# First attention of a two-layer gated cross block: roots taken by logarithm and exponential, bias rows spread by TensorE, and the opening's keys dealt out anew between VectorE and GpSimd

## The chip, the cores and the metric

The kernel runs on one core of one Trainium2 chip. The metric is the device time of one execution in microseconds (us); the time before is the median of three runs. Engines are named as the profile names them: PE (TensorE, with PEld its weight loads), DVE (VectorE), ACT (ScalarE), POOL (GpSimd) and SP (SyncE). ACTq and SPq are the instructions by which ACT and SP start transfers (DMAs).

## The reference, cut to what matters

Four sequences of 256 tokens with 256 features go through two layers. Each layer has a cross attention to a context of 1601 tokens, then a feed-forward part, each behind a gate. The change touches the first attention alone:

```python
def _ln(t, w, b):                       # over the 16 features of a head
    m = jnp.mean(t, axis=-1, keepdims=True)
    v = jnp.var(t, axis=-1, keepdims=True)
    return (t - m) * jax.lax.rsqrt(v + EPS) * w + b        # EPS = 1e-6
...
q = _ln((x @ Wq + bq).reshape(b, s1, H, HD), qn_w, qn_b)   # H = 16 heads, HD = 16
kv = jnp.concatenate([y_main @ Wk + bk, y_main @ Wv + bv], axis=-1).reshape(b, s2, H, 2 * HD)
k = _ln(kv[..., :HD], kn_w, kn_b)
v = kv[..., HD:]
ctx = _attn(qT, k.transpose(0, 2, 1, 3), v.transpose(0, 2, 1, 3))
# and a second attention to the last 16 context tokens (k_dca, v_dca), added to ctx
return ctx @ Wo + bo
```

So every key and every query of every head needs one reciprocal root of a variance. `y_main` has 1585 tokens.

## The kernel before, in words

**Stages.** By the profile's time axis: an opening that prepares the first sequence (0 to about 86 us), the first attention (to about 600 us), then the first feed-forward part, the second attention and the second feed-forward part. Each stage's instructions are issued in the order in which the program text makes them: `keep_order` ties every instruction of an engine to the one before it, on PE, ACT, DVE, POOL and SP. Nothing is rearranged later, so an instruction that waits holds up all that stands behind it on its engine. The pools' buffers add waits of their own: `ps_s` has three buffers of PSUM, `ps_m` and `ps_o` one each, the raw keys `kn` two, the split keys `kp` two.

**DMA lanes.** The transfers share eight completion counters, dealt out in turn. The ninth transfer waits, on the engine that issues it, until the first has landed, and so on.

**Keys.** The 13 tiles of 128 context tokens form the groups [0,1,2], [3,4,5], [6,7,8], [9,10,11], [12]. For a group the kernel multiplies the context by `wkv` (keys and values side by side), adds the key bias, squares (ACT), sums per head and scales to a variance (DVE), takes the root, scales the keys (POOL), and splits them into three bf16 parts by two rounds of "ACT rounds, POOL subtracts" (`split`, L341 to L352). `key_turn` (L516) then transposes the three parts into `kTs` by one DMA per tile, started by SP. Key weights, query weights and biases have their mean over a head removed first (`center`, L326), so that the products come out with zero mean.

**Roots.** In the opening `deviations` (L827) scales the variance and calls `newton_rsqrt` (L354): two integer instructions for a first guess and three rounds of three instructions, all on DVE. In the steady part `scale_heads` (L374) calls `pool_rsqrt` (L363): the two integer instructions on DVE, then three rounds of four on POOL, in the space of the squares `sq`; the scaling of the keys (L388) is POOL's too.

**The opening** (L817 to L949) makes all keys of sequence 0 at once. `first_pair` (L482) projects two tiles into one `ps_s` buffer. Groups 0 and 1 are scaled and split by POOL, group 2 is scaled by POOL and split by DVE, groups 3 and 4 by POOL. Biases and the short weight rows arrive as DMAs that write one row to all 128 partitions (`partition_broadcast`). Queries of sequence 0 are projected, scaled, staged as 64-row bf16 blocks (`stage_queries`, POOL) and transposed by a DMA (`turn_queries`). Then 16 `greatest_tile` calls find the greatest score of each query for the first slab (a sequence and four heads); `CHUNKS` cuts the keys by groups 0, 1, 2 and 3 with 4. `shift` works it into the queries, which are turned once more for the attention itself.

**The steady part** (L950 to L1024) walks 16 slabs of 14 slots. A slot runs one or two `greatest_tile` calls for the next slab (PE L647, DVE L654), one `attend_tile` (PE L686, then the exponential on ACT, L694), every second time a `weigh` (PE L708), and then whatever `plan` holds for the slot: key projections of the next sequence (PE L475, DVE L477, ACT L478), the steps of `scale_heads` and `split`, query steps, output projections. A key group that begins in slot s squares in s, sums and takes the root in s+1, scales in s+3, splits in s+4 and s+6 and is turned in s+7:

```python
for o, step in zip((1, 3, 4, 6), steps[1:]):
    place(plan, slot + o, [step])
place(plan, slot + 7, [lambda: key_turn(b, gi)])
```

Sequence 1 is prepared during the slabs of sequence 0, and so on; sequence 3 needs no successor.

Of the kernel before, what the change touches and what calls it, by code (L numbers as in the profile page):

```python
# [9 lines left out]
F32 = mybir.dt.float32  # L10
# [49 lines left out]
def tile_gated_cross_blocks(ctx: ExitStack, tc: tile.TileContext, a: dict, out: bass.AP):  # L60
# [11 lines left out]
    def load_x(t, queue=nc.sync):  # L72
        queue.dma_start(out=xs[t], in_=a["x"][t * P : (t + 1) * P, :])
# [189 lines left out]
    with ExitStack() as ph:  # L263
# [12 lines left out]
        def load_group(b, gi):  # L276
# [6 lines left out]

        wkv = wp.tile([P, 2 * D], F32, name="wkv")
        bkv = wp.tile([P, 2 * D], F32, name="bkv")
        nc.sync.dma_start(out=wkv[:, :D], in_=a["L0_xattn_Wk"])
        nc.scalar.dma_start(out=wkv[:, D:], in_=a["L0_xattn_Wv"])
        fetched = {(0, 0): load_group(0, 0)}
        nc.scalar.dma_start(out=bkv[:, :D], in_=a["L0_xattn_bk"].partition_broadcast(P))
        load_x(0)  # L290
        nc.scalar.dma_start(out=bkv[:, D:], in_=a["L0_xattn_bv"].partition_broadcast(P))
        load_x(1)
        fetched[0, 1] = load_group(0, 1)
        wq = load(wp, "wq0", [P, DC, D], a["L0_xattn_Wq"].rearrange("(c p) n -> p c n", p=P), nc.scalar)
        bq = bcast_row(wp, "L0_xattn_bq", D, nc.scalar)
        fetched.update({(0, gi): load_group(0, gi) for gi in range(2, 4)})
        hn = {
            n: bcast_row(wp, f"L0_xattn_{n}", HD0, nc.sync if "dca" in n else nc.scalar)
            for n in ("qn_w", "qn_b", "kn_w", "kn_b", "kn_dca_w", "kn_dca_b")
        }  # L300
        early = ph.enter_context(ExitStack())
        lp = early.enter_context(tc.tile_pool(name="l0last", bufs=1))
# [23 lines left out]
        def center(t3):  # L326

            g = t3.shape[1]
            sm = small.tile([P, 2 * H], F32, name="cen", bufs=2)
            nc.vector.reduce_sum(sm[:, :g], t3, axis=AX.X)  # L330
            nc.vector.tensor_scalar_mul(sm[:, :g], sm[:, :g], 1.0 / HD0)
            nc.vector.tensor_tensor(t3, t3, bc_last(sm[:, :g], HD0), ALU.subtract)
# [21 lines left out]
        def newton_rsqrt(v, y, t):  # L354

            nc.vector.tensor_scalar(y.bitcast(I32), v.bitcast(I32), 1, None, ALU.arith_shift_right)
            nc.vector.tensor_scalar(y.bitcast(I32), y.bitcast(I32), -1.0, 1597463007.0, ALU.mult, ALU.add)
            for k in range(3):
                nc.vector.tensor_tensor(t, y, y, ALU.mult)
                nc.vector.scalar_tensor_tensor(t, t, -0.5, v, ALU.mult, ALU.mult)  # L360
                nc.vector.scalar_tensor_tensor(v if k == 2 else y, t, 1.5, y, ALU.add, ALU.mult)

        def pool_rsqrt(v, y, t):  # L363

            nc.vector.tensor_scalar(y.bitcast(I32), v.bitcast(I32), 1, None, ALU.arith_shift_right)
            nc.vector.tensor_scalar(y.bitcast(I32), y.bitcast(I32), -1.0, 1597463007.0, ALU.mult, ALU.add)
            for k in range(3):
                nc.gpsimd.tensor_tensor(t, y, y, ALU.mult)
                nc.gpsimd.tensor_tensor(t, t, v, ALU.mult)
                nc.gpsimd.tensor_scalar(t, t, -0.5, 1.5, ALU.mult, ALU.add)  # L370
                nc.gpsimd.tensor_tensor(v if k == 2 else y, t, y, ALU.mult)

        def scale_heads(src, n, g):

            sq = hp.tile([P, GN * H, HD0], F32, name="sq", bufs=1)
            v = small.tile([P, GN * H], F32, name="hn_var", bufs=2)[:n, :g]

            def square():
                nc.scalar.activation(sq[:n, :g], src, AF.Square)

            def rsqrt():
                nc.vector.reduce_sum(v, sq[:n, :g], axis=AX.X)
                nc.vector.tensor_scalar(v, v, 1.0 / HD0, 1e-6, ALU.mult, ALU.add)
                space = sq.rearrange("p g e -> p (g e)")[:n]
                pool_rsqrt(v, space[:, :g], space[:, g : 2 * g])

            def scale():
                nc.gpsimd.tensor_tensor(src, src, bc_last(v, HD0), ALU.mult)  # L388

            return [square, rsqrt, scale]  # L390
# [379 lines left out]
        def plan_keys(plan, b, base, at, l):  # L770

            ctxg, kns = {}, {}
            for gi, g in enumerate(groups):

                def fetch(gi=gi):
                    ctxg[gi] = fetched.pop((b, gi), None) or load_group(b, gi)

                place(plan, base + max(at[0][0], at[gi][0] - 8), [fetch])
                for i, slot in enumerate(at[gi]):
                    place(plan, base + slot, [lambda gi=gi, i=i: key_project(b, gi, ctxg[gi], kns, i)])  # L780

                def begin(gi=gi, slot=base + l[gi]):
                    steps = key_parts(gi, kns)
                    steps[0]()
                    for o, step in zip((1, 3, 4, 6), steps[1:]):
                        place(plan, slot + o, [step])
                    place(plan, slot + 7, [lambda: key_turn(b, gi)])

                place(plan, base + l[gi], [begin])
# [25 lines left out]


        FIRST = 2 * GN  # L817
        nk0, ns0 = NKT * H * HD0, (NKT - FIRST) * H * HD0
        kn0 = kTs_f[1][:, :nk0].rearrange("p (g e) -> p g e", e=HD0)
        sq0 = kTs_f[1][:, nk0 : nk0 + ns0].rearrange("p (g e) -> p g e", e=HD0)  # L820
        v0 = lp.tile([P, (NKT + QT + 1) * H], F32, name="v0")
        qcol, dcol = FIRST * H, (NKT + QT) * H

        def kcol(t):
            return (t if t < FIRST else t + QT) * H

        def deviations(c0, c1):  # L827
            v = v0[:, c0:c1]
            nc.vector.tensor_scalar(v, v, 1.0 / HD0, 1e-6, ALU.mult, ALU.add)
            y, t = (lp.tile([P, NKT * H], F32, name=f"nr_{k}")[:, : c1 - c0] for k in "yt")  # L830
            newton_rsqrt(v, y, t)

        def square(t0, t1, base):

            for n, lo, hi in ((P, t0, min(t1, NKT - 1)), (TMAIN, NKT - 1, t1)):
                if lo < hi:
                    nc.scalar.activation(sq0[:n, (lo - base) * H : (hi - base) * H], kn0[:n, lo * H : hi * H], AF.Square)

        def sum_squares(t0, t1):
            for n, lo, hi in ((P, t0, min(t1, NKT - 1)), (TMAIN, NKT - 1, t1)):  # L840
                if lo < hi:
                    nc.vector.reduce_sum(
                        v0[:n, kcol(lo) : kcol(hi - 1) + H], sq0[:n, (lo - t0) * H : (hi - t0) * H], axis=AX.X
                    )

        def parts(gi, eng):
# [4 lines left out]
            v = v0[:n, kcol(g[0]) : kcol(g[-1]) + H]  # L851
# [3 lines left out]
                [lambda: nc.gpsimd.tensor_tensor(src, src, bc_last(v, HD0), ALU.mult)] + steps + [lambda: key_turn(0, gi)]  # L855
# [9 lines left out]
        group = [parts(gi, nc.vector if gi == 2 else nc.gpsimd) for gi in range(len(groups))]  # L865
        zero_padding(vps[0])
        center(kv3[0])
        next(ln0)
        center(kv3[1])
# [11 lines left out]
        square(0, 4, 0)  # L881
        center(wq.rearrange("p c (h e) -> p (c h) e", e=HD0))
        center(bq.rearrange("p (h e) -> p h e", e=HD0))
        first_pair(4, kn0)
        square(4, FIRST, 0)
        for i in range(QT):
            query_project(0, i)
        sqq = hp.tile([P, GN * H, HD0], F32, name="sq", bufs=1)[:, : QT * H]
        nc.scalar.activation(sqq, q3, AF.Square)
        sum_squares(0, FIRST)  # L890
        nc.vector.reduce_sum(v0[:, qcol : qcol + QT * H], sqq, axis=AX.X)
        deviations(0, qcol + QT * H)
        step(group[0])
        step(group[1])
        fetched[0, 4] = load_group(0, 4)
        first_pair(6, kn0)
        step(group[0])
        nc.vector.tensor_tensor(q3, q3, bc_last(v0[:, qcol : qcol + QT * H], HD0), ALU.mult)
        affine, fold, first_split, second_split = query_parts(0)[3:]
        affine()  # L900
        first_pair(8, kn0)
        step(group[0])
        step(group[0])
        fold()
        first_split()
        first_pair(10, kn0)
        step(group[1])
        second_split()
        stage_queries(0, 0)
        turn_queries((0, 0), 0)  # L910
        first_pair(12, kn0)
        square(FIRST, NKT, FIRST)
        step(group[1])
        step(group[1])
        sum_squares(FIRST, NKT)
        deviations(qcol + QT * H, dcol)
# [15 lines left out]
        deviations(dcol, dcol + H)  # L932
        for g in GREATEST[8:12]:
            greatest_tile(0, *g)
        next(last)
# [12 lines left out]
        nc.scalar.activation(gate, gate, AF.Tanh)  # L948
        early.close()  # L949
# [19 lines left out]
        for u, (b, s) in enumerate(slabs):  # L969
# [3 lines left out]
            if s == 0 and b + 1 < B:  # L973
                plan_keys(plan, b + 1, base_slot, KEYS[b > 0], PARTS_AT[b > 0])
                iterate(plan, base_slot + 32, last_tokens(b + 1), 12)
                if b == 0:
                    plan_queries(plan, 1, base_slot, [0, 3, 9, 10], [13, 14], [15, 16, 18, 19, 20, 21, 23])
                if b + 2 < B:
                    plan_queries(
                        plan, b + 2, base_slot + NS * SLOTS, [-8, -6, -4, -3], [-2, -1], [0, 1, 3, 4, 6, 8, 10]  # L980
                    )
# [667 lines left out]
```

## Time and profile before

| what | us |
|---|---|
| median of three runs (lowest, highest) | 1640.45 (1640.38, 1642.27) |
| profiled execution, own time | 1644.6 |
| its span, first to last instruction | 1642.8 |
| PE busy in the span | 1542.2 (94%) |
| DVE, ACT, POOL busy | 1170.4, 788.0, 658.1 |
| stretch 0 to 86 us (opening), first score product of the opening | 47.44 |
| stretch 86 to 330 us: PE busy | 221.7 of 244 |
| stretch 330 to 570 us: PE busy | 227.1 of 240 |
| stretch 560 to 1643 us: PE busy | 1061.5 of 1083 |

A row of the timeline gives the start in us, the duration in us, engine, line, operation, what it writes and reads with shapes, how many instructions were merged, and in brackets the idle time before it with what ended it. "PEclk" is the granted TensorE clock, 1.00 being full. Waits are rows of "engine, what waited, <-, what it waited for: total us, times, longest".

### The profile page before, as it was taken

The page shows a single profiled execution, that of the slowest core. Times are in us where ns is not written, and L with a number is a line of the kernel's source. Part 1 is how long each engine was busy: PE and PEld are TensorE (multiplying, and loading weights), DVE is VectorE, ACT ScalarE, POOL GpSimd, SP SyncE. Part 2 cuts the span into 40 slices and gives each one's busy share as a digit, 9 for nine tenths or more (in the row PEclk, how much of TensorE's full clock was granted, in tenths as well). Part 3 has the DMA queues.
Part 4 walks back from the last instruction along what each step waited for, and adds up shares of the span by engine and source line. Part 5 has one row for each costly group of instructions (what it writes and reads, how often), then busy time and mean ns, then how long its engine had stood idle before and what let it go on. Part 6 is the DMA issues. An engine that isn't in the chain of part 4 may idle for free.

```text
span 1642.8 us, 34188 instructions
## 1 busy us (share of the span) xinstructions
PE 1542.2 (94%) x13274; PEld 924.6 (56%) x13282; DVE 1170.4 (71%) x2621; ACT 788.0 (48%) x1808; POOL 658.1 (40%) x754
## 2 busy tenths in 40 slices
PE   4598899899999999998999999999999999999998
PEld 1254454454455554445666666666666666666665
DVE  6876668767767736677777777777877777877655
ACT  2144545554555553453555444544455444454443
POOL 4534414513621215534445444444445444444410
PEclk8699899999999999999999999999999999999999
DMA  3512612430424132000000000010000000000000
GB/s 102 100 35 45 94 32 45 78 57 16 87 44 95 37 90 110 1 2 2 15 9 21 9 15 15 8 21 3 15 9 15 15 15 15 9 2 2 2 0 27
DMA packets 148466, 54.06 MB, mean 33 GB/s; under 512 B 133200, under 2 KB 143952, under 8 KB 148176
## 3 DMA queue, kind: packets, MB, share of 16 engines
q1 hardware_dynamic: 134592, 50.65, 14.6%
q10 hardware_dynamic: 13712, 1.23, 0.6%
q8 instruction: 104, 1.70, 0.4%
q14 instruction: 58, 0.48, 0.1%
HBM read 24.30 MB, written 1.05 MB: 15 GB/s over the span
## 4 chain that ended last, share of the span: by engine, by line
PE 77%; DVE 13%; ACT 3%; issue 2%; POOL 2%; DMA 1%; ACTq 0%; SPq 0%; DVEq 0%; POOLq 0%
PE ps_o L1426 21%; PE ps_sc L1363 20%; PE ps_s L686 6%; PE ps_s L647 6%; PE ps_o L708 5%; DVE mxs L654 4%; PE ps_y L1444 4%; PE ps_m L1352 3%; PE ps_m L475 2%; PE ps_v L1186 2%; ACT pr L1378 1%; PE ps_a L1200 1%; PE ps_g L1557 1%; PE ps_x L1131 1%; PE ps_y L1582 1%
## 5 line engine op out<-in xcount | busy, mean ns | idle before, releaser
L1413 POOL TENSOR_TENSOR pr<-pr,rs 128x1604 f32<-128x1604 f32 x128 | 364.2, 2867 | 434.9 <-DMA rs<-ws 393.2
L1426 PE MATMUL ps_o<-pT,cx 128*128 128x256 f32 x1664 | 372.2, 381 | 7.8 <-DVE pT L1419 7.8
L1370 DVE CUSTOM_DVE_ANT_0 pr<-ps_sc,mk 128x401 f32<-128x401 f32 x512 | 294.6, 576 | 95.0 <-PE ps_sc L1363 56.2
L1363 PE MATMUL ps_sc<-ctxT,qT 128*32 128x401 f32 x4096 | 359.5, 502 | 0.4 <-DVE nm L1370 0.4
L1378 ACT ACTIVATE pr<-pr,nm 128x401 f32<-128x401 f32 x512 | 321.3, 629 | 71.0 <-DVE nm L1370 70.3
L1426 PEld LDWEIGHTS ps_o<-pT,cx 128*128 128x128 f32 x1664 | 318.0, 191 | 52.2 <-DVE pT L1419 8.5
L654 DVE TENSOR_REDUCE mxs<-ps_s 128x2 f32<-128x768 f32 (+1 forms) x256 | 245.9, 979 | 78.5 <-PE ps_s L647 77.9
L694 ACT ACTIVATE e<-ps_s 128x1024 f32<-128x1024 f32 (+1 forms) x224 | 214.7, 963 | 176.0 <-PE ps_s L686 161.5
L1419 DVE STREAM_TRANSPOSE pT<-pr 128x1664 f32<-128x1664 f32 x128 | 242.9, 1899 | 4.9 <-POOL pr L1413 4.7
L1363 PEld LDWEIGHTS ps_sc<-ctxT,qT 128*32 128x32 f32 x4096 | 126.2, 110 | 204.4 <-issue 119.5
L647 PE MATMUL ps_s<-kT,qTs 64*128 64x384 bf16 (+1 forms) x1536 | 177.6, 346 | 40.4 <-DMA qTs<-qp 18.1
L686 PE MATMUL ps_s<-qTs,kT 64*128 64x256 bf16 x2496 | 176.1, 272 | 11.0 <-DVE mxs L654 11.0
L686 PEld LDWEIGHTS <-kT 64*128 64x128 bf16 x2496 | 125.8, 95 | 57.5 <-issue 23.6
L647 PEld LDWEIGHTS <-qTs 64*128 64x128 bf16 x1536 | 67.0, 97 | 138.4 <-issue 91.4
L708 PE MATMUL ps_o<-e,vp 128*32 128x256 f32 x1664 | 112.8, 390 | 0.0
L1395 ACT ACTIVATE ws<-ws 32x32 f32<-32x32 f32 x64 | 14.6, 228 | 194.3 <-DVE ws L1394 194.3
L1436 ACT COPY ao<-ps_o 128x256 f32<-128x256 f32 x64 | 23.9, 373 | 152.5 <-PE ps_o L1426 141.3
L1378 ACT ACTIVATION_READ_ACCUMULATOR pr<-pr,nm 128x1 f32 x512 | 95.4, 186 | 0.0
L1444 PE MATMUL ps_y<-vo,ao 128*128 128x256 f32 x256 | 73.3, 409 | 2.1 <-ACT ao L1436 2.1
L1444 PEld LDWEIGHTS ps_y<-vo,ao 128*128 128x128 f32 x256 | 43.9, 191 | 46.5 <-ACT pr L1378 39.9
L708 PEld LDWEIGHTS ps_o<-e,vp 128*32 128x32 f32 x1664 | 44.6, 110 | 43.0 <-issue 25.6
L1352 PE MATMUL ps_m<-xnT,aq 128*128 128x256 f32 x256 | 65.8, 380 | 0.0
(288 smaller groups left out, 1553.9 us busy)
## 6 DMA issues: line engine op xcount, KB each, us to landing
ctxT<-in_ctxT_dram SPq DMA_DIRECT2D x4, 800.5 KB, 8.0
ctxg<-in_ctxT_dram SPq DMA_DIRECT2D x16, 192.0 KB, 3.2
kT<-in_L_xattn_Wq_dram SPq DMA_DIRECT2D x4, 512.0 KB, 3.5
wo<-in_L_xattn_Wo_dram SPq DMA_DIRECT2D x4, 512.0 KB, 4.5
bq<-nm SPq DMA_DIRECT2D x128, 2.0 KB, 1.7
bq<-nm ACTq DMA_DIRECT2D x128, 2.0 KB, 2.0
rs<-ws SPq DMA_DIRECT2D x128, 1.0 KB, 1.9
rs<-ws ACTq DMA_DIRECT2D x128, 1.0 KB, 1.8
```

Source lines behind the costliest of these rows:

```text
L647: nc.tensor.matmul(ps[:, k, :w], lhsT=qT[rows, j, i, r, :], rhs=kT[rows, 2 * s + r, c0 : c0 + w], start=j == 0, stop=j == NP - 1,)
L654: nc.vector.tensor_reduce(greatest_of[u][:, i, 2 * r : 2 * r + 2, n], ps[:, :, :w], AX.X, ALU.max)
L686: nc.tensor.matmul(ps[:, k, jj * S : (jj + 1) * S].rearrange("p (i q) -> p i q", i=QT), lhsT=kT[rows, 2 * s + r // 2, (j + jj) * P : (j + ...
L694: nc.scalar.activation(e[:, :, : nj * S], ps[:, :, : nj * S], AF.Exp)
L708: nc.tensor.matmul(summed[u][(r + k) * W : (r + k + 1) * W, :S], lhsT=vps[b % 2][:, j + jj, h * VW : h * VW + W], rhs=made[u, j, r][:, k, ...
L1363: nc.tensor.matmul(ps[i * TQ : (i + 1) * TQ, :KS], lhsT=queries[u][:, t * TQ : (t + 1) * TQ], rhs=ctxT[b][:, i * KS : (i + 1) * KS], start ...
L1370: nc.vector.tensor_tensor_reduce(out=prs[u % 3][:, t, :KS], in0=ps[:, :KS], in1=masks[b], scale=-1.0, scalar=3.0e38, op0=ALU.add, op1=ALU. ...
L1378: nc.scalar.activation(p, p, AF.Exp, bias=found[u][:, 0, t : t + 1], scale=-1.0, accum_out=found[u][:, 1, t : t + 1])
L1413: nc.gpsimd.tensor_tensor(p, p, bc_last(factors[:, ts], KS), ALU.mult)
L1419: nc.vector.transpose(pTs[u % 2][:, ts].rearrange("p t k -> p (t k)"), prs[u % 3][:, ts].rearrange("p t k -> p (t k)"))
L1426: nc.tensor.matmul(po[:, u % 2], lhsT=contexts[b][:, k, :], rhs=pTs[u % 2].rearrange("p t (k q) -> p t k q", q=TQ)[:, :, k, :], start=k == ...
L1444: nc.tensor.matmul(ys[b][:, i], lhsT=outs[u][:, i * P : (i + 1) * P], rhs=vo[:, h, :], start=(h, i) == (0, 0), stop=(h, i) == (H - 1, QT - 1),
```

## The change

All of it lies in the first attention.

- The activation table set that holds logarithm and exponential together is loaded as ACT's first instruction, and once more after the `Tanh` of the gates.
- `newton_rsqrt` and `pool_rsqrt` are gone. `log_root` takes Ln and then Exp with scale -0.5 on ACT; `newton` does one round of three instructions on DVE.
- A group's steps in the steady part become square (s), variance (s+1, DVE), root (s+2, ACT), one Newton round on DVE with the scaling on POOL (s+3), and the rest as before. The root's scratch is no longer the squares' space. For queries, a step is put in the same way.
- The biases of key, value and query and four short rows are loaded into one row on one partition (seven DMAs of ACT's queue), and spread to all partitions by two matmuls with a row of ones (512 and 320 columns); DVE centres the key bias from PSUM, ACT copies the rest out. Query weights and query bias lie in one tile and are centred together.
- The second x tile moves from SP's queue to ACT's; the order of the opening's loads changes.
- In the opening, groups 0 and 1 are scaled and split by DVE alone, groups 2, 3 and 4 by POOL alone; squares, sums and roots of groups 0, of the queries, of group 1 and of the rest are taken in four portions (before: groups 0 and 1 with the queries, then the rest); the last 24.5 KB of keys are fetched after the first queries are turned.

```diff
+        nc.scalar.preload_act_table_set("natural_log_exp_and_others")
...
+        def load_row(at, name):
+            n = a[name].shape[0]
+            nc.scalar.dma_start(out=row[:, at : at + n], in_=a[name].unsqueeze(0))
...
-        nc.scalar.dma_start(out=bkv[:, :D], in_=a["L0_xattn_bk"].partition_broadcast(P))
+        load_row(0, "L0_xattn_bk")
+        load_row(D, "L0_xattn_bv")
         load_x(0)
-        nc.scalar.dma_start(out=bkv[:, D:], in_=a["L0_xattn_bv"].partition_broadcast(P))
-        load_x(1)
+        load_x(1, nc.scalar)
         fetched[0, 1] = load_group(0, 1)
-        wq = load(wp, "wq0", [P, DC, D], a["L0_xattn_Wq"].rearrange("(c p) n -> p c n", p=P), nc.scalar)
-        bq = bcast_row(wp, "L0_xattn_bq", D, nc.scalar)
+        load_row(2 * D, "L0_xattn_bq")
+        nc.scalar.dma_start(out=wq, in_=a["L0_xattn_Wq"].rearrange("(c p) n -> p c n", p=P))
+        for i, n in enumerate(small_rows):
+            load_row(3 * D + i * HD0, f"L0_xattn_{n}")
...
+        def log_root(v, y):
+            nc.scalar.activation(y, v, AF.Ln)
+            nc.scalar.activation(y, y, AF.Exp, scale=-0.5)
+        def newton(v, y, t):
+            nc.vector.tensor_tensor(t, y, y, ALU.mult)
+            nc.vector.scalar_tensor_tensor(t, t, -0.5, v, ALU.mult, ALU.mult)
+            nc.vector.scalar_tensor_tensor(v, t, 1.5, y, ALU.add, ALU.mult)
...
-                    for o, step in zip((1, 3, 4, 6), steps[1:]):
+                    for o, step in zip((1, 2, 3, 4, 6), steps[1:]):
...
-                [lambda: nc.gpsimd.tensor_tensor(src, src, bc_last(v, HD0), ALU.mult)] + steps + [lambda: key_turn(0, gi)]
+                [lambda: eng.tensor_tensor(src, src, bc_last(v, HD0), ALU.mult)] + steps + [lambda: key_turn(0, gi)]
...
-        group = [parts(gi, nc.vector if gi == 2 else nc.gpsimd) for gi in range(len(groups))]
+        group = [parts(gi, nc.vector if gi < 2 else nc.gpsimd) for gi in range(len(groups))]
...
+        spread = [ps_m.tile([P, 512], F32, name="ps_m"), ps_o.tile([P, 512], F32, name="ps_o")]
+        for i, ps in enumerate(spread):
+            n = min(512, row.shape[1] - i * 512)
+            nc.tensor.matmul(ps[:, :n], lhsT=ones[:1, :], rhs=row[:, i * 512 : i * 512 + n], start=True, stop=True)
+        center(kv3[1], bias3[:, :, :HD0])
+        nc.scalar.copy(bkv.rearrange("p (h e) -> p h e", e=2 * HD0)[:, :, HD0:], bias3[:, :, HD0:])
+        nc.scalar.copy(bq, spread[1][:, :D])
+        nc.scalar.copy(hn_rows.rearrange("p i e -> p (i e)"), spread[1][:, D : D + len(small_rows) * HD0])
...
+        sum_squares(0, GN)
+        rooted(0, cut)
         first_pair(4, kn0)
...
+        polish(0, cut)
+        step(group[0])
...
         nc.scalar.activation(gate, gate, AF.Tanh)
+        nc.scalar.preload_act_table_set("natural_log_exp_and_others")
```

## The prediction

> **What bounds the kernel now.** I read the page first: the busy strip, the granted clock and the chain of work that ended last.
>
> ```profile
> PE   4598899899999999998999999999999999999998
> PEclk8699899999999999999999999999999999999999
> PE 77%; DVE 13%; ACT 3%; issue 2%; POOL 2%; DMA 1%; ACTq 0%; SPq 0%; DVEq 0%; POOLq 0%
> ```
>
> One slice is 41 us. PE carries the chain except in the first two slices and, a little, in slices 4 to 8. So a gain elsewhere counts only where PE waits. For the steady part I read PE's waits in the stretch 140 to 200, then the timeline around them.
>
> ```profile
> PE ps_m L475 <- ACT vp L478: 5.9, 2, 3.6
> PE ps_s L647 <- DVE mxs L654: 2.3, 1, 2.3
> ```
>
> ```profile
> 157.30 0.27 POOL L368 TENSOR_TENSOR sq<-sq 128x48 f32<-128x48 f32 x1 [0.82 <-DVE sq L366]
> ...
> 161.42 1.80 POOL L619 COPY qp<-qn 128x192 bf16<-128x192 bf16 x6
> 163.17 1.64 POOL L350 TENSOR_TENSOR kp<-kn,kp 128x768 bf16<-128x768 f32 x1
> ...
> 164.85 0.42 DVE L477 TENSOR_TENSOR kn<-ps_m,bkv 128x256 f32<-128x256 f32 x1 [5.74 <-POOL kp L350]
> ...
> 165.73 2.08 PE L475 MATMUL ps_m<-wkv,ctxg 128*128 128x512 f32 x2 [3.62 <-ACT vp L478]
> ```
>
> POOL works its twelve root instructions from 157.3 to 161.4, then the query copies, then the split that frees a key buffer. DVE, ACT and PE stand behind it in a row. The window table shows what follows; its columns end with clock, DMA share and GB/s.
>
> ```profile
> 162.00:166.00 4.00, 0.38 (x5) 0.27 (x2) 1.15 (x2) 0.69 (x2) 4.00 (x7) 0.78 0.00 0
> 166.00:170.00 4.00, 4.00 (x20) 1.14 (x22) 1.49 (x4) 1.28 (x3) 0.78 (x2) 0.50 1.28 167
> ```
>
> After the stall PE runs at half clock for about 4.8 us. The opening is bound by DVE, POOL and SP's queue:
>
> ```profile
> 9.76 1.28 ACT L499 ACT_TABLE_LOAD   x1 [9.76 <-DMA bc_L_xattn_qn_b<-in_L_xattn_qn_b_dram]
> ...
> 10.01 0.69 DVE L493 TENSOR_TENSOR kT<-ps_s,bkv 128x512 f32<-128x512 f32 x1
> ...
> 27.51 1.68 DVE L898 TENSOR_TENSOR qraw<-qraw,v 128x512 f32<-128x512 f32 x1
> ...
> 43.72 1.42 SPq L629 DMA_TRANSPOSE qTs<-qp  x1
> ...
> 46.92 20.62 SPq L520 DMA_TRANSPOSE kT<-kp  x9
> ...
> 47.44 3.06 PE L647 MATMUL ps_s<-kT,qTs 64*128 64x384 bf16 x18 [18.11 <-DMA qTs<-qp]
> ```
>
> Nine key transposes leave one after the other (about 1.35 us each), the last tile's follows at 67.64, and the last quarter of score products starts at 71.24, 3.6 us after that issue. I use 71.24 as the opening's clock hand: what stands there later, the whole kernel gets later, since shift, turn and attention follow it in order.
>
> **Steady part: what goes.** The change removes 18 calls (15 key groups, 3 query sets) of twelve POOL instructions, 4.2 us each by the row above (157.3 to 161.4). POOL is not the bound, so I count only PE's stalls that lead back to it:
> - 165.7: 3.62 stall. Without the root POOL copies the queries at once (156.5 to 158.5) and ends L350 near 160.1; PE wants the buffer at 162.1. All goes, and with it 2.4 us lost to the half clock: -6.0.
> - 188.3: 2.34 stall plus 1.7 us of half clock. DVE's small L383 took 1.44 us there (0.19 elsewhere), behind POOL's L346 (185.10 to 186.74), itself late by the root. L346 moves forward about 2 us; part of the overlap may stay. 4.0 less 0.8 kept: -3.2.
> - 261 and 397: PE waited 2.78 and 2.77 for L756, behind L549, which took 1.98 us beside POOL's key scaling instead of 0.69. The scaling now comes a slot later, after the Newton round, so 1.3 of each goes; at 397 also 3.0 of half clock (windows 395 to 405 at 0.64 and 0.68): -5.6.
> - 313 and 452: 1.78 and 0.41 twice, ACT waiting for POOL's L388 that waited for the root. 0.3 kept each: -3.8.
>
> Sum -18.6. The stall of 2.29 at 148.7 (DVE busy with query folding) stays.
>
> **Steady part: what comes.** Ln and Exp of 48 columns are not in the trace. Nearest rows are 0.23 us (L1395, 32x32) and 0.41 (L586, 256 columns): two of 0.25 a call, 9 us of ACT in all, where ACT is half idle. DVE trades two integer instructions (0.19 each) for three of about 0.2. New is a wait: the Newton round stands in DVE's queue in slot s+3 and needs the Exp of s+2, which stands behind that slot's exponential (1.02); behind the round wait the next score maximum, then PE by way of `ps_s`. That exponential runs while PE does the next score products and DVE their maximum, so mostly the root is there. Bounds: nothing, to 0.55 (both ACT instructions) on each of 18 = 10 us; I take 3.2, nearer nothing. Steady part: **-15.4**.
>
> [...]
>
> **Opening, start.** ACT's table load moves in front of its first DMA: 1.28 us, so the value weights leave at 2.1 instead of 0.80. The small rows are short, but the second spread matmul needs all of them, and stands before the first keys in PE's queue. Their DMAs go through the shared lanes: ACT's query weights wait for the second key load, the row kn_b waits for the query weights. The second key load took 5.8 before; it now leaves at 2.2 among fewer bytes and lands near 6.7. The query weights (256 KB; rows 3.5 and 6.4) land near 9.6, and kn_b about 2 us later (2 KB rows 1.7, 8 KB rows 3.1): 11.7, bounds 10 and 15. Then spread 0.9, two key matmuls at low clock 3.0: first key addition on DVE at 15.7 against 10.01. Hidden before that: the second x tile (it now waits for the first keys, lands near 8.2, and its normalisation is done by 10.5) and ACT's three copies out of PSUM (done by 13.4).
>
> **Opening, DVE.** From there: key addition, normalisation, second addition 2.3; query weights and bias centred 2.15 (rows 0.42 and 0.69 scaled by width); sums 1.1; two query projections 3.4 (waiting for PE); Newton round 0.7; group 0 scaled and split, 3 x 1.03 (0.68 per 512 columns scaled) with two ACT roundings between, 6.2 with what fits in between; query root to affine 3.5; additions and folding 2.8; split with ACT 3.4, group 1's sums inside. That is 25.6, and some 2.5 of waits between: the last query part is ready at 43.8 (before: 42.0) and copied at 44.6; the turn is issued at 44.65 against 43.72. So DVE wins back 3.9 of the 5.7 us: one Newton round for three (11 instructions of 128 columns, 3.3 us, go), and no POOL beside it (L898, L544, L545 took 1.7 to 1.9 for 0.69).
>
> [...]
>
> **Opening, the moved fetch.** This is the costliest step. The last 24.5 KB of keys are now fetched behind the query turn in SP's queue. Issue at 46.1 (44.65 + 1.42); landing 3.1 (its row) to 3.3 (85.71 to 89.0, also behind a turn): 49.4; matmul 1.1; DVE's addition ends at 50.9. In DVE's order group 1's Newton round stands behind it, so DVE idles about 6 us from 44.5. Then group 1: round 0.7, scaling 1.03, ACT 0.83, 1.03, ACT (the squares of the rest, 1.8, stand between) 0.83, 1.03: 57.5. Sums 2.3, root 0.6, round 0.9: 61.5. Before, the last variance was done at 50.27.
>
> **Opening, POOL and SP.** POOL scales and splits groups 2 and 3 in turn: group 2 is its fifth job, 2 x 1.5 + 2 x 1.64 + 1.64 plus gaps = 8.1: 69.6. Six transposes of 1.36: 77.8; 3.65 to land: **81.5 against 71.24, +10.2**. Before, DVE had group 2 ready at 59.26. Bounds: +3 (rows at 10, fetch in 1.7, nothing else late) and +14 (rows at 15).
>
> The second table load beside the Tanh falls where ACT idles 13 us: nothing. The transposes of groups 0 and 1 leave early and wait for nobody.
>
> **Sum.** 10.2 - 15.4 = -5.2. The profiled execution (1644.6, 1.8 more than its span) would take 1639.4; against the median of the runs, 4.15 lower, **1635.2**.
>
> **Rivals.**
> - *The opening costs little* (25%): the fetch lands before DVE is through with group 1's sums, rows land at 10, opening +3: -12.4, 1628. For it: DVE's chain saves 4 us. Against: the queue order.
> - *Slower* (20%): the roots sit on the chain. If ACT's Exp comes late by 0.8 us at each of 18 rounds, DVE hands 14.4 instead of 3.2 to PE: +6, 1646.5. It decides from 0.5 us a call on. Against: ACT is busy 25 of 50 us.
> - *Stalls only move* (15%): the next wait takes half the gain (-9 instead of -15.4): +1, 1641.7. For it: DVE is busy 39 of 60 us there.
> - *Not what it says*: Ln and Exp reload tables. 36 loads of 1.28 would cost ACT 46 us; the order of ACT's queue holds none between the gates and the end of this stage, so under 1%.
>
> Forecast 40%. Range 1626 to 1646: from below the first rival to the second. About 0.2% (3.3 us) is what a measurement tells from no change. Faster by more: two thirds of the forecast (27), the first rival (25), a fifth of the third (3): 55%. Within: the rest of these two, 25%. Slower: the second, 20%.
>
> **What will show it.** Right: no wait of L475 near 166, no half clock after it; the last quarter's products near 81; a DVE gap of 5 to 6 us ahead of the 49-row key addition; POOL below 610 us busy. Wrong: score maxima waiting for ACT's Exp at every group; the last quarter before 75; first key addition before 13.

## The result, and the profile after

The changed kernel takes 1634.7 us (median of four runs, 1634.5 to 1635.1); beside it the kernel before took 1641.4 (1640.4 to 1644.3). The ratio is 0.9957, 95% interval 0.9940 to 0.9974: faster by 0.4%. The profiled execution took 1634.7 with a span of 1632.9, against 1644.6 and 1642.8, so 9.9 us of span went. By medians it is 6.7: the profiled execution of the kernel before was slower than its median by 3.

The page first: busy times, PE's busy strip, and the shares of the chain that ended last.

```profile
PE 1540.5 (94%) x13286; PEld 923.2 (57%) x13286; DVE 1158.9 (71%) x2625; ACT 799.1 (49%) x1859; POOL 594.3 (36%) x534
...
PE   4389999999999999989999999999999999999998
...
PE 80%; DVE 11%; ACT 3%; issue 2%; POOL 2%; DMA 2%; SPq 0%; ACTq 0%; DVEq 0%; POOLq 0%
```

Slices 4, 5 and 8 rose from 8 to 9; slices 2 and 3 fell from 5 and 9 to 3 and 8. So the steady part won and the opening lost. POOL has 64 us less to do. The two kernels can be cut at ACT's first exponential of the attention (L694 before, L702 after): 88.92 before, 98.15 after. From there to the end of the span it is 1553.9 against 1534.8 us. So in this pair of traces the opening cost **+9.2** and the rest brought **-19.1**. In 1083 us at the end PE is busy 1061.5 before and 1063.0 after: nothing there changed much.

The steady part, at the place of the old stall of 3.62 us, in the timeline of the changed kernel (line numbers have moved: L359 is the old L346, L363 the old L350, L485 the old L477):

```profile
162.48 1.64 POOL L359 TENSOR_TENSOR kn<-kn,kp 128x768 f32<-128x768 f32 x1 [1.42 <-ACT kp L358]
...
164.12 1.79 POOL L627 COPY qp<-qn 128x192 bf16<-128x192 bf16 x6
165.83 0.24 ACT L369 ACTIVATE hn_y<-hn_var 128x48 f32<-128x48 f32 x1
...
166.01 1.64 POOL L363 TENSOR_TENSOR kp<-kn,kp 128x768 bf16<-128x768 f32 x1
166.11 0.24 ACT L370 ACTIVATE hn_y<-hn_y 128x48 f32<-128x48 f32 x1
167.69 0.42 DVE L485 TENSOR_TENSOR kn<-ps_m,bkv 128x256 f32<-128x256 f32 x1 [0.94 <-POOL kp L363]
168.03 0.20 DVE L374 TENSOR_TENSOR hn_t<-hn_y 128x48 f32<-128x48 f32 x1
```

POOL goes from the first subtraction to the query copies and to the second subtraction without the 4.2 us of root between. DVE still waits for it, 0.94 instead of 5.74 us, and PE's next projection no longer stands behind. The root took 0.5 us of ACT, and DVE's Newton round (L374) found it ready. The same stretch by windows of 20 us, before and then after (columns: stretch, length, busy time and count of PE, PEld, DVE, ACT, POOL; then clock, DMA share, GB/s):

```profile
160.00:180.00 20.00, 16.05 (x154) 7.34 (x150) 10.59 (x19) 8.33 (x13) 11.00 (x23) 0.83 0.45 71
180.00:200.00 20.00, 17.13 (x209) 9.89 (x210) 13.41 (x25) 11.50 (x18) 10.95 (x26) 0.91 0.59 84
```

```profile
160.00:180.00 20.00, 18.79 (x218) 9.37 (x212) 14.83 (x26) 14.01 (x22) 11.46 (x15) 1.00 0.38 60
180.00:200.00 20.00, 16.83 (x222) 9.97 (x221) 15.00 (x30) 12.68 (x23) 6.53 (x6) 1.00 0.70 101
```

PE got through 440 matmuls instead of 363, at full clock. (The stretch is the same in time, not in work: the changed kernel reaches the first subtraction at 162.48, the kernel before at 154.84.)

The opening, in the timeline of the changed kernel:

```profile
0.80 1.28 ACT L284 ACT_TABLE_LOAD   x1 [0.80 <-PEq L1662]
0.83 0.41 ACTq L302 DMA_DIRECT2D wkv<-in_L_xattn_Wv_dram  x1
...
11.45 1.40 PE L879 MATMUL ps_o<-row,ones 1*128 1x320 f32 x2 [5.41 <-DMA row<-in_L_xattn_kn_b_dram]
...
16.60 0.69 DVE L501 TENSOR_TENSOR kT<-ps_s,bkv 128x512 f32<-128x512 f32 x1 [8.14 <-PE ps_s L496]
...
43.45 1.43 SPq L637 DMA_TRANSPOSE qTs<-qp  x1
44.99 0.79 SPq L281 DMA_DIRECT2D ctxg<-in_ctxT_dram  x1
...
49.38 0.42 DVE L501 TENSOR_TENSOR kT<-ps_s,bkv 49x256 f32<-49x256 f32 x1 [6.43 <-PE ps_s L496]
...
79.45 2.60 PE L655 MATMUL ps_s<-kT,qTs 64*128 64x433 bf16 x24 [1.98 <-DMA kT<-kp_last]
```

The second spread matmul waits for the row kn_b, and DVE idles 8.14 us before the first key addition. Later the fetch leaves behind the query turn, and DVE idles 6.43 us. The last quarter of score products starts at 79.45 instead of 71.24.

### The profile page after: what moved, and what is told of

It reads as the page before. It is cut to its first block, busy times and chain, and to the rows that moved or that the text cites. A ratio compares the mean times of both kernels' runs of the same rounds, so it can differ in the third digit from the quotient of the medians.

```text
span 1632.9 us, 33955 instructions
## 1 busy us (share of the span) xinstructions
PE 1540.5 (94%) x13286; PEld 923.2 (57%) x13286; DVE 1158.9 (71%) x2625; ACT 799.1 (49%) x1859; POOL 594.3 (36%) x534
## 4 chain that ended last, share of the span: by engine, by line
PE 80%; DVE 11%; ACT 3%; issue 2%; POOL 2%; DMA 2%; SPq 0%; ACTq 0%; DVEq 0%; POOLq 0%
PE ps_o L1450 21%; PE ps_sc L1387 20%; PE ps_s L694 7%; PE ps_s L655 6%; PE ps_o L716 5%; PE ps_y L1468 4%; DVE mxs L662 3%; PE ps_m L1376 3%; PE ps_m L483 2%; PE ps_v L1210 2%; PE ps_a L1224 1%; ACT pr L1402 1%; PE ps_g L1581 1%; PE ps_x L1155 1%; PE ps_u L1581 1%
## 5 line engine op out<-in xcount | busy, mean ns | idle before, releaser
L702 ACT ACTIVATE e<-ps_s 128x1024 f32<-128x1024 f32 (+1 forms) x224 | 214.7, 964 | 165.5 <-PE ps_s L694 150.8
L694 PE MATMUL ps_s<-qTs,kT 64*128 64x256 bf16 x2496 | 174.0, 270 | 10.3 <-DVE mxs L662 10.1
L694 PEld LDWEIGHTS <-kT 64*128 64x128 bf16 x2496 | 125.1, 94 | 55.8 <-issue 22.7
L1416 DVE TENSOR_REDUCE low<-bq 32x8 f32<-32x32 f32 x64 | 12.4, 194 | 77.4 <-DMA bq<-nm 77.4
```

Of the source, the lines that this page charges most:

```text
L694: nc.tensor.matmul(ps[:, k, jj * S : (jj + 1) * S].rearrange("p (i q) -> p i q", i=QT), lhsT=kT[rows, 2 * s + r // 2, (j + jj) * P : (j + ...
L702: nc.scalar.activation(e[:, :, : nj * S], ps[:, :, : nj * S], AF.Exp)
```

## The experiments

**The theory** after this reading: two independent sums. The opening loses 9 us, by two delays on one chain (short rows at its head, late fetch at its tail). The steady part gains 18 to 19 because the key groups' roots left POOL. **Rivals:** the opening's loss lies in the new division of DVE and POOL; the steady gain is luck of the clock or needs the new opening; the root's new wait costs something. Times are medians; ratios are to the kernel before, run beside them on the same chip (its medians there were 1642 to 1644). The last two columns cut each kernel's one profiled execution at the first exponential, as above.

| kernel | us | ratio (95% interval) | first exponential at | from there to the end |
|---|---|---|---|---|
| before | 1641.4 | 1 | 88.92 | 1553.9 |
| changed | 1634.7 | 0.9957 (0.9940 to 0.9974) | 98.15 | 1534.8 |
| e2 new opening alone | 1652.6 | 1.0052 (1.0036 to 1.0069) | 100.07 | 1552.6 |
| e3 new roots in the steady part alone | 1625.3 | 0.9888 (0.9874 to 0.9903) | 85.37 | 1538.0 |
| e1 changed, fetch early | 1628.2 | 0.9907 (0.9893 to 0.9922) | 91.93 | 1536.5 |
| e4 changed, short rows late | 1628.7 | 0.9908 (0.9893 to 0.9923) | 92.56 | 1533.0 |
| e5 both | 1622.4 | 0.9879 (0.9864 to 0.9894) | 84.08 | 1535.6 |
| e6 changed, root a slot later | 1639.1 | 0.9981 (0.9971 to 0.9991) | 101.00 | 1540.6 |
| e7 as e5, group 2 on DVE | 1622.9 | 0.9876 (0.9859 to 0.9892) | 88.90 | 1534.6 |
| e8 as e7, group 2 ahead of the maxima | 1621.4 | 0.9870 (0.9854 to 0.9887) | 83.53 | 1536.8 |
| e10 changed, query roots on POOL | 1632.8 | 0.9938 (0.9919 to 0.9957) | 97.77 | 1536.2 |
| e11 changed, key roots on POOL | 1654.0 | 1.0066 (1.0049 to 1.0083) | 96.98 | 1553.7 |

The last column settles the steady part. The three kernels with the key roots on POOL (before, e2, e11) need 1552.6 to 1553.9 us; the eight with the new key roots a slot ahead need 1533.0 to 1538.0, on average 17.7 less, with the old opening and with the new. The first exponential is less steady: five traces of the changed opening have it between 96.98 and 101.00, two of the old one at 85.37 and 88.92.

### The two halves: new opening alone (e2), new roots alone (e3)

The first is the changed kernel with the old `pool_rsqrt` and the old slots in the steady part:

```diff
-            def root():
-                log_root(v, y)
+                space = sq.rearrange("p g e -> p (g e)")[:n]
+                pool_rsqrt(v, space[:, :g], space[:, g : 2 * g])
...
-                    for o, step in zip((1, 2, 3, 4, 6), steps[1:]):
+                    for o, step in zip((1, 3, 4, 6), steps[1:]):
```

> Changed opening, but the steady part with the roots of the kernel before: twelve POOL instructions, two integer instructions on DVE, steps in slots s, s+1, s+3, s+4, s+6. Theory A (opening and steady part add up): first exponential near 98.15 as changed, POOL near 658 us busy, and the stalls of 3.62, 2.34 and 2.78 return: 1641.4 + 9.2 = 1650.6. Rival B (part of the opening's loss is made good later, because the steady part has slack that takes it in): 1645 or less.

The second is the kernel before with these edits the other way round, and the table set loaded behind the Tanh.

> Opening of the kernel before, but the steady part with roots by Ln and Exp, one Newton round, and the table set loaded after the gates' Tanh. Theory A (the two add up, and the steady part is worth what the spans say: 9.2 lost and 9.9 gained in all): first exponential near 88.9, POOL near 594 us busy, 1641.4 - 19.1 = 1622.3. By the prediction's steady term, -15.4: 1626. Rival B (the gain needs the new opening, whose later start puts the slots in another phase, or is luck of the half clock): 1630 or more.

Measured: 1652.6 and 1625.3, against 1643.5 for the kernel before beside them. The opening alone costs 9.1, the roots alone bring 18.3; their sum is -9.2. The changed kernel lies 6.7 under the kernel before as measured beside it, 8.8 under this 1643.5; the kernel before varies by that much, and by spans it is 9.9. By these differences theory A holds for both. In itself e3's time lies nearer to the 1626 of the prediction's term than to A's 1622.3, and its first exponential came at 85.37, not near 88.9: in its trace 3.5 of the 19.4 us of span gained lie in an opening whose code is the old one, and 15.9 behind it. Rival B of each is out: nothing of the opening's loss is given back later, and the gain needs no new opening. In e2 the old stalls are back in the timeline, 11 us later than before:

```profile
176.91 2.07 PE L490 MATMUL ps_m<-wkv,ctxg 128*128 128x512 f32 x2 [3.58 <-ACT vp L493]
```

### Which roots: queries on POOL (e10), keys on POOL (e11)

Both are the changed kernel; `scale_heads_pool` is the old function with its old slots, used for one kind of call.

```diff
         def query_parts(b):
...
-                scale_heads(q3, P, QT * H)
+                scale_heads_pool(q3, P, QT * H)
```

> Changed kernel (1634.7), but the roots of the three query sets of the steady part on GpSimd again, with the slots of the kernel before; the 15 key groups keep Ln and Exp. It splits the steady part's gain. Theory A (the prediction's places: the stall of 3.62 and the half clock after it belong to the first query set, the other stalls to key groups): the stall near 165.7 (here some 9 us later by the opening) returns, +6 to +8: 1640.5 to 1642.5. Rival B (any call is worth the same, 3 of 18): +3: 1637.7. Rival C (the key groups alone matter): within 1 us of 1634.7.

```diff
         def key_parts(gi, kns):
...
-            return scale_heads(src, n, len(g) * H) + split(
+            return scale_heads_pool(src, n, len(g) * H) + split(
...
-                    for o, step in zip((1, 2, 3, 4, 6), steps[1:]):
+                    for o, step in zip((1, 3, 4, 6), steps[1:]):
```

> Changed kernel (1634.7), but the roots of the 15 key groups of the steady part on GpSimd again, in the slots of the kernel before; the three query sets keep Ln and Exp. With query sets' roots alone on GpSimd the time was 1632.8, with both on GpSimd 1652.6. Theory A (the gain is the key groups' alone: the root's 4.2 us on GpSimd stands ahead of the query copies and the split that frees a key buffer): 1651 to 1653, the stalls of 3.6, 2.3 and 2.8 us are back. Rival B (the two kinds stand in each other's way on GpSimd, so that taking away either is enough): 1634 to 1638. Rival C (a mix): 1642 to 1646.

Measured: 1632.8 (four runs between 1628.8 and 1635.7) and 1654.0. The three query calls are worth nothing that these runs show, the 15 key calls all of it: behind the first exponential e10 takes 1536.2 like the changed kernel, e11 1553.7 like the kernel before. The expectation of e10 named the wrong owner of the 3.62 stall: the root quoted in the prediction has 128x48 operands, which is a key group (three tiles of 16 heads), while a query set has 32 columns. In e11 it is back in full:

```profile
170.89 0.29 POOL L386 TENSOR_TENSOR hn_var<-sq 128x48 f32<-128x48 f32 x1
171.12 0.21 POOL L654 MEMSET qp<- 128x24 bf16 x1
171.17 1.79 POOL L657 COPY qp<-qn 128x192 bf16<-128x192 bf16 x6
172.92 1.65 POOL L363 TENSOR_TENSOR kp<-kn,kp 128x768 bf16<-128x768 f32 x1
...
175.49 2.07 PE L513 MATMUL ps_m<-wkv,ctxg 128*128 128x512 f32 x2 [3.62 <-ACT vp L516]
```

The key root's last instruction, the query copies, the split, and behind them PE: the order that the prediction read.

### What the new wait costs (e6)

```diff
-                    for o, step in zip((1, 2, 3, 4, 6), steps[1:]):
+                    for o, step in zip((1, 3, 3, 4, 6), steps[1:]):
```

The query plans are changed in the same way.

> Changed kernel with Ln and Exp of the steady part one slot later, directly ahead of the Newton round and the scaling in slot s+3 (query sets in the same way), so that DVE reaches the Newton round before ACT, whose 1.02 us exponential stands ahead, has the root. It measures what the wait costs that the prediction put at 3.2 us in all (bounds 0 and 10). Theory A (DVE has slack; a slot ahead the wait cost nothing, and without that slot it costs a little): DVE waits of 0.5 to 1.5 us at the Newton round's first instruction, total +2 to +5 against the changed kernel's 1634.7. Rival B (the rival of the prediction, DVE hands such a wait on to PE each time): 18 times 0.8, +12 to +15. Rival C (DVE's slack swallows all): within 1 us of 1634.7.

Measured: 1639.1 (ten runs between 1637.1 and 1643.4), so +4.4 on the changed kernel: theory A. Behind the first exponential its trace, of the slowest of the ten, takes 1540.6, 4.9 more than the eight others; its mean clock was 0.977, the changed kernel's 0.980, and how much of the 4.9 is the clock isn't shown. The waits of this kernel in the stretch 90 to 590 have a row that the changed kernel's lack (total us, times, longest):

```profile
DVE hn_t L374 <- ACT hn_y L370: 15.9, 15, 1.7
```

So between a quarter and a third of DVE's 15.9 us reached the end of the kernel. With a slot between root and Newton round the wait is nil: the changed kernel's 18 Newton rounds had no idle time ahead of them.

### The late fetch (e1) and the short rows (e4)

```diff
         rooted(*qall)
+        fetched[0, 4] = load_group(0, 4)
         first_pair(6, kn0)
...
         turn_queries((0, 0), 0)
-        fetched[0, 4] = load_group(0, 4)
```

> Changed kernel (1634.7), with the fetch of the last 24.5 KB of keys put back in front of group 0's turn and the first queries' turn in SP's queue; all else as changed. Theory A (the fetch behind the query turn is the costliest step of the opening): the fetch leaves before 38 us instead of 44.99, DVE's gap of 6.43 us ahead of the 49-row key addition goes, group 1 and the last variance come about 6 us earlier (last variance near 53.5 instead of 59.47), the last quarter of score products near 73.5 instead of 79.45; total 1634.7 - 6 = 1628.7. Rival B (DVE's serial order and POOL's second group set the end, the fetch is hidden behind DVE's work): the gap is filled by other waits, the last quarter stays above 78; total 1633.5 to 1634.7.

```diff
         for i, ps in enumerate(spread):
             n = min(512, row.shape[1] - i * 512)
-            nc.tensor.matmul(ps[:, :n], lhsT=ones[:1, :], rhs=row[:, i * 512 : i * 512 + n], start=True, stop=True)
+            if i == 0:
+                nc.tensor.matmul(ps[:, :n], lhsT=ones[:1, :], rhs=row[:, i * 512 : i * 512 + n], start=True, stop=True)
...
-        nc.scalar.copy(bq, spread[1][:, :D])
-        nc.scalar.copy(hn_rows.rearrange("p i e -> p (i e)"), spread[1][:, D : D + len(small_rows) * HD0])
...
         first_pair(2, kn0)
         for _ in ln0:
             pass
+        n = row.shape[1] - 512
+        nc.tensor.matmul(spread[1][:, :n], lhsT=ones[:1, :], rhs=row[:, 512:], start=True, stop=True)
+        nc.scalar.copy(bq, spread[1][:, :D])
+        nc.scalar.copy(hn_rows.rearrange("p i e -> p (i e)"), spread[1][:, D : D + len(small_rows) * HD0])
```

GpSimd's scaling of the two query rows moves behind them too.

> Changed kernel (1634.7), with the second spread matmul and ACT's copies of query bias and short rows moved behind the first two pairs of keys in PE's and ACT's queues; the first keys then wait for key and value biases alone. Theory A (the short rows hold the first keys): first key addition near 9.5 us instead of 16.60; DVE reaches the query turn 4 to 6 us earlier (issue near 40), the fetch behind it too; last quarter near 75; total 1629 to 1631. Rival B (query weights, whose DMA stands in the same queue, and DVE's amount of work hold the chain anyway): first key addition early, but the query turn no more than 2 us earlier; total 1632.7 or more.

Measured: 1628.2 and 1628.7, -6.5 and -6.0. In e1 the fetch leaves at 18.88, and the last key addition follows the one before it with no gap (the two merged into one row); the last quarter starts at 74.76:

```profile
43.84 1.00 DVE L501 TENSOR_TENSOR kT<-ps_s,bkv 128x512 f32<-128x512 f32 x2
...
45.57 0.96 DVE L861 TENSOR_TENSOR kT<-kT,v 128x768 f32<-128x768 f32 x1
```

In e4 the first key addition comes at 9.86, and the whole chain with it, but the gap ahead of the last stays:

```profile
9.86 0.69 DVE L501 TENSOR_TENSOR kT<-ps_s,bkv 128x512 f32<-128x512 f32 x1 [1.30 <-PE ps_s L496]
...
44.90 0.42 DVE L501 TENSOR_TENSOR kT<-ps_s,bkv 49x256 f32<-49x256 f32 x1 [6.60 <-PE ps_s L496]
```

The fetch stands behind the query turn, so it moved with the queries. Both expectations A hold, and the rivals, which had DVE's work or POOL's second group hold the end, don't. (These times and the changed kernel's 1634.7 were taken on different occasions; the first exponentials, 6.2 and 5.6 earlier, say the same.)

### Both at once (e5)

> Changed kernel with both edits at once: the early fetch and the late second spread. Each alone gave about -6 us (1628.2 and 1628.7). Theory A (two separate delays on one chain: the rows hold its head, the fetch holds its tail; with both gone DVE runs through): first key addition near 9.9, query turn near 39, no gap of 6 us ahead of the 49-row key addition, last variance near 47.5, last quarter near 68; total near 1622.5. Rival B (both alone reach a common floor, the SP queue's row of transposes or POOL's two groups): total 1627 to 1628.5, last quarter still near 74.

Measured: 1622.4, -12.3 on the changed kernel: the two add up. Last variance done at 49.1, last quarter at 68.25. So the new division of DVE and POOL is not what the opening lost by: it is unchanged here. With head and tail free, the new opening is 2.9 us ahead of the old one with the same roots (e3, 1625.3), but that isn't shown: the two intervals overlap almost wholly.

### Group 2 on DVE (e7), and ahead of the maxima (e8)

```diff
-        group = [parts(gi, nc.vector if gi < 2 else nc.gpsimd) for gi in range(len(groups))]
+        group = [parts(gi, nc.vector if gi < 3 else nc.gpsimd) for gi in range(len(groups))]
```

> The kernel with both edits, and group 2 scaled and split by DVE instead of POOL (so groups 0 to 2 on DVE, 3 and 4 on POOL, side by side). Theory A (with head and tail free, POOL's two groups in a row, 9.4 us, are next on the chain; side by side they take some 6 to 7): group 2's turns start 3 us earlier, last quarter near 65; total 2 to 4 us under the kernel with both edits. Rival B (the nine transposes in SP's queue, 1.36 each, bind by then, or DVE and POOL slow each other where they work side by side): within 1 us of the kernel with both edits.

Measured: 1622.9, no gain on e5, as rival B said. Group 2 was ready at 57.2, against 57.0 on POOL: in DVE's order its last subtraction stood behind four score maxima.

```profile
50.74 1.27 DVE L359 TENSOR_TENSOR kT<-kT,kp 128x768 f32<-128x768 f32 x1 [0.90 <-ACT kp L358]
51.93 3.54 DVE L662 TENSOR_REDUCE mxs<-ps_s 128x2 f32<-128x768 f32 x4
55.39 1.78 DVE L363 TENSOR_TENSOR kp<-kT,kp 128x768 bf16<-128x768 f32 x1
```

So e8 puts both remaining steps of group 2 (split and turn) ahead of the maxima:

```diff
             step(group[3])
+        for _ in range(2):
+            step(group[2])
         for g in GREATEST[:4]:
             greatest_tile(0, *g)
         for _ in range(2):
-            step(group[2])
             step(group[3])
```

> The kernel with both edits and group 2 on DVE (1622.9), but all of group 2's split ahead of the first score maxima in DVE's order; before, its last subtraction stood behind four maxima and began at 55.39 us. Theory A (that order took away what the division of labour gave): group 2 is ready near 54 instead of 57.2, its turns start there, last quarter of score products near 66 instead of 69.34; total 1619 to 1620.5. Rival B (VectorE and GpSimd side by side, the same instructions 1.27 and 1.78 us instead of 0.96 on DVE and 2.19 instead of 1.49 on POOL, eat it; or the first quarters' maxima now come late and hold PE): 1622 or more.

Measured: 1621.4, between the two expectations, and not to be told from e5 and e7 (intervals 0.9854 to 0.9887 and 0.9864 to 0.9894). Group 2 was ready at 54.35 and the last quarter started at 66.79, 1.5 us ahead of e5, but the first exponential only 0.5 us ahead (83.53 against 84.08): the first maxima now come late on DVE and hold the first score products, which wait 9.51 us for them. DVE's order paid with one what it won with the other. e5 and e8 beat both kernels: 1.2 to 1.3% under the one before.

## Why the prediction was right

The forecast, 1635.2, is 0.5 from the measured 1634.7. That it is so near is partly luck. It is a sum of two terms of opposite sign: the steady part brought 2 to 3 more than forecast and the opening cost about 1 less, so the two errors add up. What hid them is the time that the forecast started from: 1640.45, a median of three runs, while the kernel before took 1641.4 beside the changed kernel and 1642.2 to 1643.8 beside the experiments. The change was forecast at -5.2 and measured at -6.7 by medians, at -9.9 by spans.

- **Steady part: -15.4 predicted, about -18 measured** (17.7 by the table's last column; e3 18.3; e2 against the changed kernel 17.9). The mechanism is the one named. Place by place in the two timelines: the 3.62 stall and its half clock went (6.0, as predicted; the windows give 5.4 us of half clock behind the stall, not 4.8, so 0.3 more); 2.34 became 1.06 and its half clock went (3.0; predicted 3.2); 2.78 and 2.77 became 1.39 each, and the half clock at 397 went (5.8; predicted 5.6); 1.78 and 1.77 went and with them the two of 0.41 and 0.42 (4.4; predicted 3.8). The 2.29 stall stayed, at 1.95.
- Mis-sized there, first: **the new root wait, 3.2 predicted, nothing measured.** No Newton round of the changed kernel's steady part waits; e6 shows what the slot between is worth, 4.4 us. Rival "slower", 0.8 us handed on 18 times, would have been too dear even without it: 15.9 us of waits cost 4.4.
- Second, not in the list: the stalls of 1.02 (294.6, 433.6) and 0.70 (304.0, 443.0) went too, 3.4 us; a new one of 1.48 at 192.75 (the last tokens' `pd`) came. With these the list comes to 21, 2 more than the 19.1 of this pair of traces; where the rest went isn't shown.
- Misread, though the sum doesn't use it: 4.2 us of root on POOL is the price of a call with 48 columns, not of all 18. In e3 POOL is busy 56 us less than before, 3.1 a call.
- **Opening: +10.2 predicted, +9.2 measured at the first exponential and +8.2 at the last quarter in this pair of traces, 9.1 by e2's median.** The two causes are those named, and e1 and e4 price them: 6.5 for the fetch behind the query turn, 6.0 for the short rows ahead of the first keys. They come to 12.5, so the rest of the new opening should bring some 3; the traces leave that open (first exponential at 83.5 to 88.9 in e5, e7 and e8, at 85.4 and 88.9 with the old opening).
- Mis-sized there: **the table load delays nothing.** The prediction put ACT's first DMA at 2.1; it left at 0.83, during the load. The short rows were late all the same, since the second matmul of the spread, at 11.45, waits for kn_b (predicted landing 11.7), the two spread instructions took 1.40 (0.9 assumed), and the key matmuls behind them 3.7 (3.0 assumed): first key addition 16.60, predicted 15.7.
- The rest of the chain ran 1 to 2 us ahead of the working: query turn issued at 43.45 (predicted 44.65), last key addition done at 49.8 (50.9), last variance at 59.5 (61.5), last quarter 79.45 (81.5). DVE's instructions on 768 columns took 0.96 instead of the 1.03 scaled from 512, and the fetch landed 2.3 us after its issue instead of 3.3. The gap on DVE was 6.43, as said.
- The signs given in advance all came: no long wait of the key projection near 166 and no half clock, last quarter near 81, DVE gap of 5 to 6, POOL at 594.3 (below 610).
- **The half-clock terms (2.4, 1.7, 3.0) held, but such a term is no fixed price.** In the kernel before half clock came with or right behind the stalls of 3.62, 2.34 and 2.77 at 397 (the clock was 0.50 from 165 to 171, 189 to 191 and 397 to 403), and not with the 2.78 at 261 (1.00). In e2 the same places have 0.84 in the window 160 to 180 (stall 3.58), 0.93 and 0.92 from 180 to 220 (2.33), 0.91 from 400 to 420 (2.77) and 1.00 from 260 to 280 (2.77 too); e11 has 0.84 from 160 to 180 (3.62). Both outcomes show at the stall that stayed. The same stall of 1.94 or 1.95, ahead of a key projection of sequence 1, in e3 and then in the changed kernel, with the two windows of 2 us behind it:

```profile
144.79 1.13 PE L479 MATMUL ps_m<-wkv,ctxg 128*128 128x512 f32 x2 [1.94 <-ACT vp L482]
```

```profile
146.00:148.00 2.00, 2.00 (x18) 1.11 (x14) 1.93 (x6) 0.96 (x2) 0.08 (x1) 0.50 0.00 0
148.00:150.00 2.00, 2.00 (x24) 0.72 (x22) 0.65 (x1) 1.59 (x2) 1.42 (x1) 0.65 0.03 8
```

```profile
156.43 1.12 PE L483 MATMUL ps_m<-wkv,ctxg 128*128 128x512 f32 x2 [1.95 <-ACT vp L486]
```

```profile
157.00:159.00 2.00, 1.61 (x18) 0.76 (x18) 1.97 (x5) 1.34 (x4) 0.00 (x0) 1.00 0.00 0
159.00:161.00 2.00, 2.00 (x34) 1.00 (x30) 1.25 (x3) 1.81 (x3) 1.44 (x1) 1.00 0.04 8
```

In e3 the clock (third column from the end) fell to 0.50 behind it; in the changed kernel it stayed at 1.00. The fall shows in e1 (1.95; 0.50 from 153 to 155) and e10 (1.85; 0.50 from 158 to 160) as well. Within e2 a stall of 2.77 left the clock at 1.00 at 272, and one of 2.77 at 410 was followed by 0.61 and 0.54. So a stall of some 2 us cost up to 1.7 us more in e3 (2 us at 0.50 and 2 at 0.65), e1 and e10, and nothing more in the changed kernel: not a fixed price. The changed kernel's trace, with no half clock at all in this stage, was lucky against e3's and e10's, which have 6.8 us of it each. What decides between the two isn't shown: PE was busy 2.06 of the 4 us around the stall in e3 (142 to 146) and in the changed kernel (153 to 157) alike.

Left open: whether the opening's other edits bring 3 us and which of them, why one opening's first exponential varies by 4 us between traces, and how far the clock's two outcomes widen the spread between executions.

## What to carry to other kernels

Add up opening and steady part apart, and look for a gain in each with the other's loss undone: here a change of -0.4% held one of -1.1% and two avoidable delays of 6 us each. In queues of fixed order, ask of every moved load or bundled wait what it now stands behind: a 24.5 KB fetch behind a turn that waits for the longest chain, and first keys behind rows that only the queries need, cost two thirds of what the roots saved (12.5 of 18.3 us). And where a result crosses engines, a slot of other work between producer and consumer can make the wait free: here it took 15.9 us of waits to none.

## What the runs showed of the hardware

- In the changed kernel ACT's DMA issues went out while its table load ran: load 0.80 to 2.08, issues at 0.83, 1.28 and 1.83.
- The clock behind the same stall fell or stayed (above). In e1 1.95 us of stall brought 0.50, as 1.94 did in e3. By windows of 1 us between 102 and 590 us, the kernel before has three stretches of half clock (the loss counted as time at 0.50), of 6.8, 3.4 and 6.8 us, from 164, 188 and 396, and the changed kernel none; by windows of 2 us those of e1 (from 151), e3 (146 and 183) and e10 (156 and 194) come to 3.4 each. A stretch of 3.4 us at half clock costs up to 1.7.
- In e8 three instructions took longer beside one of the other engine that had begun earlier. On POOL and then on DVE:

```profile
48.76 2.19 POOL L861 TENSOR_TENSOR kT<-kT,v 128x768 f32<-128x768 f32 x1 [9.77 <-DVE v L376]
51.89 1.64 POOL L359 TENSOR_TENSOR kT<-kT,kp 128x768 f32<-128x768 f32 x1 [0.94 <-ACT kp L358]
```

```profile
48.64 0.96 DVE L861 TENSOR_TENSOR kT<-kT,v 128x768 f32<-128x768 f32 x1
50.49 1.27 DVE L359 TENSOR_TENSOR kT<-kT,kp 128x768 f32<-128x768 f32 x1 [0.90 <-ACT kp L358]
52.66 1.69 DVE L363 TENSOR_TENSOR kp<-kT,kp 128x768 bf16<-128x768 f32 x1 [0.90 <-ACT kp L362]
```

POOL's 2.19 is 1.49 (its usual time) and 0.70, and DVE's instruction had 0.84 to go when it started. DVE's 1.69 is 0.96 and 0.73, and POOL's had 0.87 to go; its 1.27 is 0.96 and 0.31, with 0.46 to go. In these rows the later one took longer by most of what the earlier one had left; whether it stood still first or ran slower throughout isn't shown. L898 in the kernel before is alike: POOL's first key scaling ran from 27.15 to 28.64, L898 from 27.51 to 29.19, which is its own 0.69 and 0.99, with 1.13 of the scaling to go.
- One opening runs differently from execution to execution. e3 has the opening code of the kernel before, but its first score products start at 45.31 instead of 47.44; in it the third pair of keys kept DVE waiting 0.60 instead of 2.12 us, and the first exponential came 3.5 earlier.
